# Gates of a graph network formed in pairs: the second 16 nodes added as differences on the first sums

## The chip, the cores and the metric

The kernel runs on one core of one Trainium2 chip. The core has a matmul engine (PE), a vector engine (DVE), an activation engine (ACT), a general engine (POOL), and a queue engine (SP) that issues most transfers. PE writes PSUM banks of 128 x 512 f32; DVE and ACT read and write PSUM and SBUF; POOL works on SBUF here. The metric is the device time of one execution in microseconds (us). Before the change it is 1396.1 us, the median of three runs (1394.9 to 1398.25).

## The reference, cut to what matters

The whole program is a stack of graph layers and feed-forward layers. Only the first part is touched, two graph layers, each followed by a gate between 256 nodes (8 graphs of 32) and 64 queries per graph, with 768 features:

```python
def _gate(h, q, Wg, bg, Wq, bq):
    B, L, F = q.shape                      # 8, 64, 768
    h3 = h.reshape(B, N, F)                # N = 32 nodes of a graph
    hg = einsum('bnf,gf->bng', h3, Wg[:, :F])
    qg = einsum('blf,gf->blg', q, Wg[:, F:]) + bg
    attn = sigmoid(hg[:, :, None, :] + qg[:, None, :, :])
    qi = einsum('bnlf,blf->bnf', attn, q)
    alpha = sigmoid(h3 @ Wq[:, :F].T + qi @ Wq[:, F:].T + bq)
    return alpha * tanh(qi) + (1 - alpha) * h3
```

For every graph, node, query and feature a sum of a node term and a query term goes through a sigmoid, is multiplied by the query and summed over the 64 queries.

## The kernel before, in words

**Units.** Features lie on the partitions. A unit is one graph `b` and one block `f` of 128 features; there are 48 in a layer. For a unit the gates are a tile of 128 x (32 nodes x 64 queries), f32, one of five buffers that `wtile` shares with a few other tiles. The first four graphs come graph by graph, the last four feature block by feature block.

**Forming a gate.** The sums are made by PE. `split3` cuts a projection into three bf16 parts that add up to the f32 value. `ga` holds two parts of a graph's 64 query terms in 128 rows; `gb` holds the third part in 64 rows and below it the three parts of 16 nodes in 48 rows, 112 rows in all, once for each half `u` of the nodes. Constant matrices of zeros and ones (`sela`, `selb`) pick a query and a node for each of 512 columns. `form` (L792) does two steps, one for each half: four matmuls (L798, L799) into a pair of PSUM banks `acc` (two such pairs rotate), then a sigmoid (L805) of 128 x 1024 into the gate tile.

**After it.** Units go by threes. For the first two of a triple POOL multiplies by the queries (L825); for the third ACT copies the 64 query columns into the PSUM bank `qy` ahead of its sigmoids (L822) and DVE multiplies (L832). `total` (L810) is DVE's sum over the queries. DVE's block for a triple is: the sum of the second unit of the triple before, the sum of the first unit of this one, the multiplication of the third unit, its sum.

**Work beside.** At each step of `form` the generator `beside` issues one more matmul over 384 columns in f32 on PE: in layer 0 the projections of later graphs (`q_terms` L582, `node_terms` L604), the alpha terms (`alpha_nodes` L632, `alpha_gates` L673), and products for the next layer (`z_beside` L644); in layer 1 less. From unit 22 of layer 0 on, the second step of a unit issues two. `alpha_gates` goes on only when the reductions that it needs were emitted five steps ago. What follows a projection (casts on ACT, L570 and L572, subtractions on DVE, L571 and L573, transfers by SP, L590 to L621) is emitted by `flush` a given number of steps later. `blend` puts three pieces for the first half of the nodes among the steps: transposes (L701), a tanh (L702), a subtraction (L705), sigmoids (L707), a multiplication and an addition (L711, L712). `z_beside` reads the blended nodes.

**Order.** `pin` keeps every instruction of this stage in program order on its engine, so a waiting instruction holds all behind it. Transfers on SP are placed by a planner. A node projection goes to `gb` over a DRAM tile (`rows`), apart from graph 0, which is copied from SBUF.

Of the kernel before, what the change touches and what calls it, by code (L numbers as in the profile page):

```python
# [18 lines left out]
P = 128  # L19
N = 256  # L20
NC = 2
D = 768
# [31 lines left out]
def graph_ffn_stack_kernel(ctx: ExitStack, tc: tile.TileContext, a: dict, out: bass.AP):  # L54
# [386 lines left out]
    with tc.tile_pool(name="g0", bufs=1) as g0, tc.tile_pool(name="g0t", bufs=2) as g0t, \  # L441
# [92 lines left out]


        gate_ctx = ExitStack()
        gt = gate_ctx.enter_context(tc.tile_pool(name="gate", bufs=1))
        ga = gt.tile([P, NB, D], BF16, name="ga")
        gb = gt.tile([P, 2, NB, D], BF16, name="gb")
        sela = gt.tile([P, 8, LQ], BF16, name="sela")  # L540
        selb = gt.tile([P, 2, 8, LQ], BF16, name="selb")
        nc.vector.tensor_copy(sela[0:64], ident[0:64, None, 0:64].to_broadcast([64, 8, LQ]))
        nc.vector.tensor_copy(sela[64:P], ident[64:P, None, 64:P].to_broadcast([64, 8, LQ]))
        id16 = ident[64:P, 64:P].rearrange("p (t n) -> p t n", t=4)
        nodes = gt.tile([P, 16], F32, name="nodes")
        nc.vector.tensor_tensor(nodes[64:P], id16[:, 0, :], id16[:, 1, :], OP.add)
        nc.vector.tensor_tensor(nodes[64:P], nodes[64:P], id16[:, 2, :], OP.add)
# [29 lines left out]
        def q_terms(w, c, i):  # L577

            fs = slice(i * 384, (i + 1) * 384)
            ps = side_bank("ps_qg")[:, :384]  # L580
            for k in range(KD):
                pin(nc.tensor.matmul(ps, qT[:, k, c * P:(c + 1) * P], w(k, i * 384, (i + 1) * 384),  # L582
                                     start=k == 0, stop=k == KD - 1))
# [12 lines left out]
            yield  # L596

        def node_terms(w, hT, c, i):

# [3 lines left out]
            for k in range(KD):  # L603
                pin(nc.tensor.matmul(ps, hT[:, k, c * P:(c + 1) * P], w(k, i * 384, (i + 1) * 384),  # L604
                                     start=k == 0, stop=k == KD - 1))
# [71 lines left out]
        def blend(hT, qiT, nT, qy, c):  # L677
# [67 lines left out]
        for layer in range(2):  # L745
# [3 lines left out]
            if layer == 0:  # L749
                run(q_terms(w_gb, 0, 0), q_terms(w_gb, 0, 1))  # L750
            gT = feature_tile("gT")
            for o in range(KD):
                ps = bank("ps_rgcn")[:, :N]
# [11 lines left out]
            nT = feature_tile("nT")  # L765
            qy = one_bank("qy", "ps_qy")
            if layer == 0:
# [3 lines left out]
                side[0] = 0  # L771
                beside = chained(lambda: q_terms(w_gb, 1, 1), lambda: node_terms(w_ga, gT, 1, 0),
                                 lambda: q_terms(w_gb, 2, 0), lambda: q_terms(w_gb, 3, 0),
                                 lambda: node_terms(w_ga, gT, 1, 1), lambda: q_terms(w_gb, 2, 1),
                                 lambda: q_terms(w_gb, 3, 1), lambda: pause(2), lambda: alpha_nodes(wa, gT, 0),
# [6 lines left out]
            else:  # L782
                run(node_terms(w_ga, gT, 1, 0))
                side[0] = 0
                beside = chained(lambda: node_terms(w_ga, gT, 1, 1), lambda: pause(10), lambda: alpha_nodes(wa, gT, 0),
                                 lambda: alpha_gates(wb, qiT, 0), lambda: blend(gT, qiT, nT, qy, 0),
# [4 lines left out]

            def form(b, f):  # L792
                fs = slice(f * P, (f + 1) * P)
                g = wtile("gate", (NPB, LQ))
                for u in range(2):
                    acc = acc2("gate_acc")
                    for i in range(2):
                        pin(nc.tensor.matmul(acc[:, i, :], ga[:, b, fs], sela, start=True, stop=False))  # L798
                        pin(nc.tensor.matmul(acc[:, i, :], gb[0:112, u, b, fs], selb[0:112, i], start=False, stop=True))  # L799
                    steps[0] += 1  # L800
                    next(beside, None)
                    if layer == 0 and u and n >= half * KD - 2:
                        next(beside, None)
                    flush()
                    pin(nc.scalar.activation(g[:, u * 16:(u + 1) * 16, :].rearrange("p n l -> p (n l)"),  # L805
                                             acc.rearrange("p a n -> p (a n)"), AF.Sigmoid, bias=bg[:, f:f + 1]))
                return g

# [8 lines left out]
            for n, (b, f) in enumerate(units):  # L817
                q = qT[:, f, b * LQ:(b + 1) * LQ]
                if n % 3 == 2:
                    at = (n // 3) % 4 * LQ  # L820
                    q_ps = qy[:, at:at + LQ]
                    pin(nc.scalar.copy(q_ps, q))  # L822
                g = form(b, f)
                if n % 3 != 2:
# [1175 lines left out]
```

## Time and profile before

| what | us |
|---|---|
| median of three runs (lowest to highest) | 1396.1 (1394.9 to 1398.25) |
| profiled execution, its own time | 1399.24 |
| its span, first to last instruction | 1397.2 |
| gate stage, layer 0: first POOL multiplication to last reduction | 140.13 to 310.48 |
| gate stage, layer 1: the same | 390.61 to 543.44 |
| busy over the span: PE, DVE, ACT, POOL | 1250.9, 672.2, 477.1, 360.5 |

In the rows of the page a group reads: line, engine, operation, output<-input with partitions x elements, count, then busy time and mean length in ns, then the idle time of the engine just before the group and what ended most of it. In a timeline a row starts with start and length in us, and the idle time before it stands in brackets with its releaser. In a row of busy time by stretch each engine has its busy us and its count; the clock of PE (1.00 is full), the share of the transfer engines and GB/s end the row.

### The profile page before, as it was taken

To read this page: it belongs to the slowest core of one execution; us is meant where nothing else is said; L and a number is where in the kernel's file an instruction comes from. 1 tells how busy PE (TensorE), PEld (TensorE's weight loads), DVE (VectorE), ACT (ScalarE), POOL (GpSimd) and SP (SyncE) were. 2 spreads that over 40 slices of the span, in tenths; PEclk is the share of its full clock that TensorE was granted. 3 is DMA by queue.
4 is the path that set the end of the run, shared out by engine and by line. 5 is a ranking of instruction groups with operands and counts; after the bars stand their busy time and mean duration, and the time that the engine had idled before them with its cause. 6 is when DMAs were issued, how large, how long until landed. Compare 5 with 4: busy or idle time off the path is not lost. (4 is left out here: it accounts for less than half of the span.)

```text
span 1397.2 us, 13979 instructions
## 1 busy us (share of the span) xinstructions
PE 1250.9 (90%) x5088; PEld 768.1 (55%) x5088; DVE 672.2 (48%) x1278; ACT 477.1 (34%) x826; POOL 360.5 (26%) x200
## 2 busy tenths in 40 slices
PE   7999999989998885799899978987879999878998
PEld 4567445446743432665545554545567545467854
DVE  4330899871079998315446271058262101365033
ACT  1012776551177763224114212215211111172122
POOL 1000998660089994000111201021011000100000
PEclk9999999999999996899999979998989999975989
DMA  9332160116240022150573139943019799801000
GB/s 345 115 120 95 43 183 19 68 57 237 79 125 0 0 102 77 52 198 7 192 282 128 53 110 371 364 183 102 23 63 348 291 395 401 338 1 36 32 0 23
DMA packets 78026, 197.70 MB, mean 142 GB/s; under 512 B 8828, under 2 KB 24288, under 8 KB 77824
## 3 DMA queue, kind: packets, MB, share of 16 engines
q1 hardware_dynamic: 69664, 163.06, 32.5%
q0 software_dynamic: 6576, 28.95, 5.9%
q10 hardware_dynamic: 1712, 4.72, 0.9%
q8 instruction: 44, 0.72, 0.2%
q14 instruction: 30, 0.25, 0.1%
HBM read 178.00 MB, written 15.27 MB: 138 GB/s over the span
## 5 line engine op out<-in xcount | busy, mean ns | idle before, releaser
L825 POOL TENSOR_TENSOR gate<-gate,qT 128x2048 f32<-128x2048 f32 x64 | 287.9, 4544 | 235.7 <-ACT gate L805 235.5
L805 ACT ACTIVATE gate<-gate_acc,bg 128x1024 f32<-128x1024 f32 x192 | 210.0, 1114 | 49.3 <-PE gate_acc L799 46.6
L810 DVE TENSOR_REDUCE qiT<-gate 128x32 f32<-128x2048 f32 x96 | 215.2, 2280 | 20.6 <-POOL gate L825 19.6
L798 PE MATMUL gate_acc<-sela,ga 128*128 128x512 bf16 x384 | 147.7, 385 | 24.2 <-ACT gate L805 23.8
L799 PE MATMUL gate_acc<-selb,gb 112*128 112x512 bf16 x384 | 148.0, 385 | 0.0
L1199 PE MATMUL up_acc<-w_e,xgT 128*64 128x384 f32 (+1 forms) x432 | 96.4, 489 | 0.0
L799 PEld LDWEIGHTS <-gb 112*128 112x128 bf16 x384 | 37.7, 98 | 94.6 <-issue 69.9
L832 DVE TENSOR_TENSOR gate<-gate,ps_qy 128x2048 f32<-128x2048 f32 x32 | 73.0, 2280 | 1.5 <-ACT gate L805 1.5
L1199 PEld LDWEIGHTS up_acc<-w_e,xgT 128*64 128x64 f32 (+1 forms) x432 | 46.9, 154 | 44.7 <-issue 27.3
L798 PEld LDWEIGHTS <-ga 128*128 128x128 bf16 x384 | 37.9, 99 | 48.1 <-issue 2.7
L673 PE MATMUL ps_alpha<-w_qb,qiT 128*128 128x384 f32 x96 | 42.0, 536 | 12.5 <-DVE qiT L810 12.5
L571 DVE TENSOR_TENSOR ps_hg<-ps_hg,hg 128x384 f32<-128x384 f32 x8 | 4.5, 562 | 96.7 <-ACT hg L570 96.7
L267 DVE CUSTOM_DVE_ANT_0 gat_dot<-xl,row 128x128 f32<-128x128 f32 (+2 forms) x56 | 23.8, 425 | 52.8 <-ACT xl L1577 18.9
L462 PE MATMUL ps_z<-w_rel,xT 128*128 128x384 f32 x144 | 47.9, 486 | 0.0
L1166 POOL DMA_INDIRECT yg<-ys,rows x8 | 7.6, 955 | 153.6 <-DMA w_qk<-in_L_ffn_W_qkvT 100.6
L1735 DVE TENSOR_TENSOR h<-up_acc,h 128x768 f32<-128x768 f32 x6 | 5.7, 958 | 80.1 <-PE up_acc L1199 80.1
L171 PE MATMUL ps_tr<-ident,xn 128*128 128x128 f32 x84 | 17.6, 377 | 29.0 <-DVE xn L160 14.1
L466 ACT COPY z<-ps_z 128x384 f32<-128x384 f32 x20 | 9.6, 479 | 90.2 <-PE ps_z L462 86.9
L102 PE MATMUL ps_e<-xT,w_s 128*128 128x256 f32 x144 | 36.4, 417 | 4.1 <-DVEq L1750 4.1
L632 PE MATMUL ps_alpha<-w_qa,gT 128*128 128x384 f32 x96 | 38.5, 496 | 0.7 <-ACT al L685 0.7
L1166 POOL DMA_INDIRECT xg<-table,slots x12 | 12.0, 1000 | 101.5 <-DVE gs L1640 37.7
L329 PE MATMUL ps_pt<-ident,gat_z 128*128 128x128 f32 x104 | 22.1, 344 | 16.6 <-DVE gat_s L321 16.6
(452 smaller groups left out, 2227.8 us busy)
## 6 DMA issues: line engine op xcount, KB each, us to landing
w_e<-in_L_ffn_W SPq DMA_DIRECT2D x32, 1152.0 KB, 12.4
w_rel<-in_L_gnn_W_rel SPq DMA_DIRECT2D x12, 1152.0 KB, 9.2
wi<-in_L_ffn_WiT SPq DMA_DIRECT2D x8, 1152.0 KB, 12.2
wo<-in_L_ffn_WoT SPq DMA_DIRECT2D x8, 1152.0 KB, 11.3
w_down<-in_L_ffn_W SPq DMA_DIRECT2D x8, 1152.0 KB, 11.0
w_s<-in_L_ffn_Ws SPq DMA_DIRECT2D x5, 1152.0 KB, 8.4
w_root<-in_L_gnn_W_root SPq DMA_DIRECT2D x4, 1152.0 KB, 11.3
w_ga<-in_L_gnn_WgAT SPq DMA_DIRECT2D x4, 1152.0 KB, 7.6
```

The source lines that it names most:

```text
L102: mm = nc.tensor.matmul(ps, w(k, lo, lo + P), xT[:, k, :], start=start and k == 0, stop=stop and k == kcs - 1)
L267: pin(nc.vector.tensor_tensor_reduce(t, xl[:, c, h * C:(h + 1) * C], r[:, h * C:(h + 1) * C], 1.0, 0.0, OP.mult, OP.add, accum_out=a2[:, w ...
L462: mm = nc.tensor.matmul(ps, hT[:, k, c * P:(c + 1) * P], w(k, i * 384, (i + 1) * 384), start=k == 0, stop=k == KD - 1)
L632: pin(nc.tensor.matmul(al_ps[c][i], hT[:, k, c * P:(c + 1) * P], w(k, i * 384, (i + 1) * 384), start=k == 0, stop=False))
L673: pin(nc.tensor.matmul(al_ps[c][i], qiT[:, f, c * P:(c + 1) * P], w(f, i * 384, (i + 1) * 384), start=False, stop=f == KD - 1))
L798: pin(nc.tensor.matmul(acc[:, i, :], ga[:, b, fs], sela, start=True, stop=False))
L799: pin(nc.tensor.matmul(acc[:, i, :], gb[0:112, u, b, fs], selb[0:112, i], start=False, stop=True))
L805: pin(nc.scalar.activation(g[:, u * 16:(u + 1) * 16, :].rearrange("p n l -> p (n l)"), acc.rearrange("p a n -> p (a n)"), AF.Sigmoid, bias ...
L810: pin(nc.vector.tensor_reduce(qiT[:, f, b * NPB:(b + 1) * NPB], g, AX.X, OP.add))
L825: pin(nc.gpsimd.tensor_tensor(g, g, q[:, None, :].to_broadcast([P, NPB, LQ]), OP.mult))
L832: pin(nc.vector.tensor_tensor(g, g, q_ps[:, None, :].to_broadcast([P, NPB, LQ]), OP.mult))
L1199: pin(nc.tensor.matmul(ps[at:at + n, :], xT[:, k, at:at + n], ws[r](k, lo, hi), start=start, stop=stop))
```

## The change

- A pair of units is formed together. The four steps of a pair are: first half of unit one, first half of unit two, second half of unit one, second half of unit two. Each unit keeps its own `acc` for both halves.
- The second half is no longer made from nothing. Its matmul adds, on top of the sums in PSUM, the difference between node 16 + n and node n: one matmul over 48 rows (`gd`, three bf16 parts of 16 differences) where there were two over 128 and 112 rows.
- `step_nodes` makes the node values for that on DVE before the projection (the first 16 nodes as they are, the second 16 minus the first), so `node_terms` projects these instead of `gT`. For the first half of the nodes they lie in a tile `d0`, for the second half in a part of `nT` that is not used yet.
- `gb` is kept once instead of twice; the differences go to `gd`, always by way of the DRAM tile, with rows 0 to 47 for even graphs and 64 to 111 for odd ones. A selector `seld` for rows 0 to 47 is added.
- ACT's copy of the queries stands behind the four sigmoids of a pair, not ahead of a unit's two.
- The tanh of the first blend goes to a tile of its own in SBUF (two buffers), no longer to the bank `qy`.

```diff
-        gb = gt.tile([P, 2, NB, D], BF16, name="gb")
+        gb = gt.tile([P, NB, D], BF16, name="gb")
+        gd = gt.tile([P, NB // 2, D], BF16, name="gd")
...
+        seld = gt.tile([64, 2, 8, LQ], BF16, name="seld")
...
+            nc.vector.tensor_copy(seld[:, i], nodes[0:64, i * 8:(i + 1) * 8, None].to_broadcast([64, 8, LQ]))
...
-                    for u in range(2):
-                        nc.sync.dma_start(gb[0:64, u, b, fs], parts[r, 2, :])
+                    nc.sync.dma_start(gb[0:64, b, fs], parts[r, 2, :])
...
+        def step_nodes(to, hT, c, o):
+            a, b = (t.rearrange("p (b u n) -> p b u n", b=4, u=2) for t in (hT[:, o, c * P:(c + 1) * P], to[:, o, :]))
+            nc.vector.tensor_copy(b[:, :, 0, :], a[:, :, 0, :])
+            nc.vector.tensor_tensor(b[:, :, 1, :], a[:, :, 1, :], a[:, :, 0, :], OP.subtract)
...
-                    for u in range(2):
-                        for s in range(3):
-                            nc.sync.dma_start(gb[64 + s * 16:80 + s * 16, u, 0, fs], parts[u * 16:(u + 1) * 16, s, :])
+                    for s in range(3):
+                        nc.sync.dma_start(gb[64 + s * 16:80 + s * 16, 0, fs], parts[0:16, s, :])
                 v = rows.rearrange("(j u n) s d -> u s n j d", j=4, u=2)
-                for u in range(2):
+                for s in range(3):
+                    nc.sync.dma_start(gb[64 + s * 16:80 + s * 16, c * 4 + j0:(c + 1) * 4, fs], v[0, s][:, j0:, :])
+                for o in range(2):
                     for s in range(3):
-                        nc.sync.dma_start(gb[64 + s * 16:80 + s * 16, u, c * 4 + j0:(c + 1) * 4, fs], v[u, s][:, j0:, :])
+                        nc.sync.dma_start(gd[o * 64 + s * 16:o * 64 + 16 + s * 16, c * 2:(c + 1) * 2, fs], v[1, s][:, o::2, :])
...
-                th = qy[:, at:at + 256].rearrange("p (k n) -> p k n", k=2)
+                th = (qy[:, at:at + 256] if c else gt.tile([P, 256], F32, name="th", bufs=2)).rearrange(
+                    "p (k n) -> p k n", k=2)
...
                 nc.scalar.activation(gT[:, o, :], ps, AF.Relu, bias=col(bias, o))
-            run(node_terms(w_ga, gT, 0, 0), node_terms(w_ga, gT, 0, 1))
+                step_nodes(d0, gT, 0, o)
+            run(node_terms(w_ga, d0, 0, 0), node_terms(w_ga, d0, 0, 1))
...
+            def form(pair):
+                gs = [wtile("gate", (NPB, LQ)) for _ in pair]
+                accs = [acc2("gate_acc") for _ in pair]
                 for u in range(2):
+                    for (b, f), g, acc in zip(pair, gs, accs):
+                        fs = slice(f * P, (f + 1) * P)
+                        h = slice(b % 2 * 64, b % 2 * 64 + 48)
+                        for i in range(2):
+                            if u == 0:
+                                pin(nc.tensor.matmul(acc[:, i, :], ga[:, b, fs], sela, start=True, stop=False))
+                                pin(nc.tensor.matmul(acc[:, i, :], gb[0:112, b, fs], selb[0:112, i],
+                                                     start=False, stop=True))
+                            else:
+                                pin(nc.tensor.matmul(acc[:, i, :], gd[h, b // 2, fs],
+                                                     seld[0:48, i] if b % 2 == 0 else selb[64:112, i],
+                                                     start=False, stop=True, skip_group_check=True))
+                        steps[0] += 1
                         next(beside, None)
+                        if layer == 0 and u and n >= half * KD - 2:
+                            next(beside, None)
+                        flush()
+                        pin(nc.scalar.activation(g[:, u * 16:(u + 1) * 16, :].rearrange("p n l -> p (n l)"),
+                                                 acc.rearrange("p a n -> p (a n)"), AF.Sigmoid, bias=bg[:, f:f + 1]))
+                return gs
...
+                if n % 2 == 0:
+                    pair = form(units[n:n + 2])
+                g = pair[n % 2]
                 if n % 3 == 2:
                     at = (n // 3) % 4 * LQ
                     q_ps = qy[:, at:at + LQ]
                     pin(nc.scalar.copy(q_ps, q))
-                g = form(b, f)
```

More of the change, by code (lines that the diff above doesn't have):

```diff
@@ L538, in graph_ffn_stack_kernel @@
         ga = gt.tile([P, NB, D], BF16, name="ga")
-        gb = gt.tile([P, 2, NB, D], BF16, name="gb")
+        gb = gt.tile([P, NB, D], BF16, name="gb")
+        gd = gt.tile([P, NB // 2, D], BF16, name="gd")
         sela = gt.tile([P, 8, LQ], BF16, name="sela")
         selb = gt.tile([P, 2, 8, LQ], BF16, name="selb")
+        seld = gt.tile([64, 2, 8, LQ], BF16, name="seld")
         nc.vector.tensor_copy(sela[0:64], ident[0:64, None, 0:64].to_broadcast([64, 8, LQ]))
         nc.vector.tensor_copy(sela[64:P], ident[64:P, None, 64:P].to_broadcast([64, 8, LQ]))
-        id16 = ident[64:P, 64:P].rearrange("p (t n) -> p t n", t=4)
         nodes = gt.tile([P, 16], F32, name="nodes")
-        nc.vector.tensor_tensor(nodes[64:P], id16[:, 0, :], id16[:, 1, :], OP.add)
-        nc.vector.tensor_tensor(nodes[64:P], nodes[64:P], id16[:, 2, :], OP.add)
+        for h in (slice(0, 64), slice(64, P)):
+            id16 = ident[h, h].rearrange("p (t n) -> p t n", t=4)
+            nc.vector.tensor_tensor(nodes[h], id16[:, 0, :], id16[:, 1, :], OP.add)
+            nc.vector.tensor_tensor(nodes[h], nodes[h], id16[:, 2, :], OP.add)
         for i in range(2):
@@ L591, in place, with node_terms @@
                     nc.sync.dma_start(ga[64:P, b, fs], parts[r, 1, :])
-                    for u in range(2):
-                        nc.sync.dma_start(gb[0:64, u, b, fs], parts[r, 2, :])
+                    nc.sync.dma_start(gb[0:64, b, fs], parts[r, 2, :])
             split3(ps, "qg", place)
             yield
-        def node_terms(w, hT, c, i):
+        def step_nodes(to, hT, c, o):
+            a, b = (t.rearrange("p (b u n) -> p b u n", b=4, u=2) for t in (hT[:, o, c * P:(c + 1) * P], to[:, o, :]))
+            nc.vector.tensor_copy(b[:, :, 0, :], a[:, :, 0, :])
+            nc.vector.tensor_tensor(b[:, :, 1, :], a[:, :, 1, :], a[:, :, 0, :], OP.subtract)
+        def node_terms(w, dT, c, i):
             fs = slice(i * 384, (i + 1) * 384)
@@ L603, in node_terms @@
             for k in range(KD):
-                pin(nc.tensor.matmul(ps, hT[:, k, c * P:(c + 1) * P], w(k, i * 384, (i + 1) * 384),
+                pin(nc.tensor.matmul(ps, dT[:, k, :], w(k, i * 384, (i + 1) * 384),
                                      start=k == 0, stop=k == KD - 1))
@@ L751, in graph_ffn_stack_kernel @@
             gT = feature_tile("gT")
+            d0 = wtile("d0", (KD, P))
             for o in range(KD):
@@ L765, in graph_ffn_stack_kernel @@
             nT = feature_tile("nT")
+            d1 = nT[:, :, P:]
+            for o in range(KD):
+                step_nodes(d1, gT, 1, o)
             qy = one_bank("qy", "ps_qy")
@@ L771, in graph_ffn_stack_kernel @@
                 side[0] = 0
-                beside = chained(lambda: q_terms(w_gb, 1, 1), lambda: node_terms(w_ga, gT, 1, 0),
+                beside = chained(lambda: q_terms(w_gb, 1, 1), lambda: node_terms(w_ga, d1, 1, 0),
                                  lambda: q_terms(w_gb, 2, 0), lambda: q_terms(w_gb, 3, 0),
-                                 lambda: node_terms(w_ga, gT, 1, 1), lambda: q_terms(w_gb, 2, 1),
+                                 lambda: node_terms(w_ga, d1, 1, 1), lambda: q_terms(w_gb, 2, 1),
                                  lambda: q_terms(w_gb, 3, 1), lambda: pause(2), lambda: alpha_nodes(wa, gT, 0),
@@ L782, in graph_ffn_stack_kernel @@
             else:
-                run(node_terms(w_ga, gT, 1, 0))
+                run(node_terms(w_ga, d1, 1, 0))
                 side[0] = 0
-                beside = chained(lambda: node_terms(w_ga, gT, 1, 1), lambda: pause(10), lambda: alpha_nodes(wa, gT, 0),
+                beside = chained(lambda: node_terms(w_ga, d1, 1, 1), lambda: pause(10), lambda: alpha_nodes(wa, gT, 0),
                                  lambda: alpha_gates(wb, qiT, 0), lambda: blend(gT, qiT, nT, qy, 0),
                                  lambda: pause(3), lambda: alpha_nodes(wa, gT, 1), lambda: alpha_gates(wb, qiT, 1))
-            def form(b, f):
-                fs = slice(f * P, (f + 1) * P)
-                g = wtile("gate", (NPB, LQ))
+            def form(pair):
+                gs = [wtile("gate", (NPB, LQ)) for _ in pair]
+                accs = [acc2("gate_acc") for _ in pair]
@@ L795, in form @@
                 for u in range(2):
[L796 to L802, printed above, removed]
-                        next(beside, None)
@@ L804, in form @@
[L804 to L807, printed above, removed]
+                    for (b, f), g, acc in zip(pair, gs, accs):
[11 more added lines that the diff above has]
+                        steps[0] += 1
+                        next(beside, None)
+                        if layer == 0 and u and n >= half * KD - 2:
[3 more added lines that the diff above has]
+                                                 acc.rearrange("p a n -> p (a n)"), AF.Sigmoid, bias=bg[:, f:f + 1]))
```

## The prediction, made before the changed kernel was run

> **What bounds the kernel now.** I read the groups of the page first, then busy time by stretch of the gate stage, then single engines around the stalls, last the matmul engine's raw order. The change touches the gate stage alone; it runs twice (layer 0 and layer 1).
>
> ```profile
> L825 POOL TENSOR_TENSOR gate<-gate,qT 128x2048 f32<-128x2048 f32 x64 | 287.9, 4544 | 235.7 <-ACT gate L805 235.5
> L805 ACT ACTIVATE gate<-gate_acc,bg 128x1024 f32<-128x1024 f32 x192 | 210.0, 1114 | 49.3 <-PE gate_acc L799 46.6
> L810 DVE TENSOR_REDUCE qiT<-gate 128x32 f32<-128x2048 f32 x96 | 215.2, 2280 | 20.6 <-POOL gate L825 19.6
> L798 PE MATMUL gate_acc<-sela,ga 128*128 128x512 bf16 x384 | 147.7, 385 | 24.2 <-ACT gate L805 23.8
> L799 PE MATMUL gate_acc<-selb,gb 112*128 112x512 bf16 x384 | 148.0, 385 | 0.0
> ```
>
> Three units (a triple) cost POOL two multiplications, 2 x 4.51 = 9.0 us; DVE three reductions and one multiplication, about 4 x 2.24 = 8.95 us; ACT six sigmoids, 6.7 us. POOL and DVE are nearly equal, so saving PE time counts only where PE is slower than 9 us a triple. Busy time by stretch (columns: PE, weight loads, DVE, ACT, POOL, clock, DMA):
>
> ```profile
> 140.00:205.00 65.00, 63.67 (x249) 31.46 (x248) 60.11 (x36) 51.59 (x63) 63.12 (x14) 1.00 0.36 110
> 205.00:238.00 33.00, 32.30 (x124) 16.41 (x123) 32.86 (x18) 22.39 (x26) 28.36 (x7) 1.00 0.18 43
> 238.00:262.00 24.00, 21.41 (x79) 10.93 (x78) 17.24 (x17) 14.16 (x22) 16.72 (x4) 0.93 0.28 99
> 262.00:310.00 48.00, 43.57 (x163) 22.23 (x161) 42.14 (x19) 28.26 (x33) 36.02 (x8) 0.99 0.12 41
> 391.00:544.00 153.00, 125.60 (x479) 57.09 (x478) 146.86 (x77) 107.45 (x123) 143.94 (x34) 0.96 0.15 48
> ```
>
> Layer 1 (last row) has POOL and DVE busy 94% and 96%: almost nothing to win. Layer 0 begins the same way (POOL 63.1 of 65), and only after 238 does POOL idle. The rest of layer 0 is where the change can pay. There, in the timeline, multiplications of a triple (L832) start 11.04 us apart (271.14, 282.18, 293.22), 2 us over POOL's pace; and around 238 to 262 the blend of the first half stalls everyone:
>
> ```profile
> 248.64 0.39 ACT L702 ACTIVATE ps_qy<-qiT 128x256 f32<-128x256 f32 x1 [4.75 <-DVE gate L832]
> ...
> 251.77 8.99 POOL L825 TENSOR_TENSOR gate<-gate,qT 128x2048 f32<-128x2048 f32 x2 [6.05 <-ACT gate L805]
> ...
> 255.38 0.42 DVE L705 TENSOR_TENSOR nT<-ps_qy,gT 128x256 f32<-128x256 f32 x1 [3.12 <-ACT ps_qy L822]
> ```
>
> The tanh writes the PSUM bank that the queries live in, so it waits for a DVE multiplication that only reads queries. DVE's idle gaps from 238 to 310 add up to 12.2 us: no more than that can be won in layer 0.
>
> **Removed: two of eight matmuls a unit.** Durations of 379 ns overlap; starts give the price:
>
> ```profile
> 160.84 0.38 PE L798 MATMUL gate_acc<-sela,ga 128*128 128x512 bf16 x1
> ...
> 161.71 0.81 PE L582 MATMUL ps_qg<-w_gb,qT 128*128 128x384 f32 x2
> ...
> 162.36 0.38 PE L798 MATMUL gate_acc<-sela,ga 128*128 128x512 bf16 x1
> ```
>
> Four gate matmuls take 161.71 - 160.84 = 0.87 us, 0.217 each; one f32 matmul of the work beside takes 0.65. A step after unit 22 averages 0.87 + 1.5 x 0.65 = 1.84, so a triple 11.04, as seen. Two matmuls less save 0.433 a unit.
>
> **Added: matmuls over 48 rows.** [...]
>
> ```profile
> 1195.87 1.45 PE L1160 MATMUL moe_acc<-w_s,gs 128*128 128x384 f32 x4
> 1197.26 0.91 PE L1162 MATMUL moe_acc<-b,cwT 9*128 9x384 f32 x2
> 1198.09 0.91 PE L1160 MATMUL moe_acc<-w_s,gs 128*128 128x384 f32 x2
> ...
> 1161.61 0.49 PE L1725 MATMUL up_acc<-b_rows,own 72*128 72x384 bf16 x2
> 1161.94 3.39 PE L1199 MATMUL up_acc<-w_e,xgT 128*128 128x384 f32 x10
> ```
>
> A record of 384 f32 columns normally takes 0.323 (2 x 0.323 = 0.65). Four before L1162 should end at 1197.16; it starts 0.10 late. Its two take 0.83 where 0.65 was due: 0.18. The pair after it reads 0.91 where the plain pair above reads 0.81: another 0.10. So a visit to a nine-row matmul costs 0.38; 72 rows (L1725, 0.33 for two of 0.16) cost nothing, and 48 lies on the nine-row side. With bf16 weights (98 ns to load against some 187 in f32) I take 0.32; bounds 0.18 (the two gaps alone) and 0.39. Every second-half step makes one visit, since work beside follows. Without the price of the rule, 24 units from 22 on would save 24 x 0.433 = 10.4 us; with it 24 x 0.113 = **-2.7 us** (bounds -6.1 and -1.0). In units 0 to 21 and in layer 1 POOL and DVE hide it: 0.
>
> **Pairs, start.** Three sigmoids run back to back from 137.93 and POOL starts at 140.13, after the second. In pairs the second sigmoid is unit 1's, so unit 0 is complete one sigmoid later: +1.1. In layer 1 likewise (390.61 now). With a small wait of the first DVE multiplication for the copy behind four sigmoids: **+2.4 us** for both; no cover, POOL and DVE being full from there on.
>
> **Pairs, first 22 units.** Splits of the projections flush every six steps: second cast (ACT), subtraction (DVE). Now four steps are emitted before DVE's block of a unit n=2 (mod 6). So at steps 18, 30, 42 two rounds of subtractions stand side by side, and the second waits for a cast that waits for the first: a cast of 0.48 plus two hops, 0.6 us of idle DVE where DVE is the bound, three times: **+1.8** (0 to 2.5). The cast stands ahead of two sigmoids on ACT, which have over 2 us of slack.
>
> **Tanh to SBUF.** Freed of the bank. It ends the 4.75 us wait above; the DVE gaps it can close are 1.98 + 3.12 in layer 0 and an ACT wait of 1.6 in layer 1. But the next item makes DVE late there anyway, so I take **-1.0 and -1.0** (bounds 0 and -6.7).
>
> **The third piece of the blend.** Counting steps: before, the last reductions of unit 22 are emitted at step 54, now with pair 26/27 at step 56, so the work beside reaches the blend two steps later. The blend's third piece (subtract, multiply, add, 1.25 us) stood at steps 71 and 72, just ahead of DVE's block for unit 35; now it is at 73 and 74, behind it. Two matmuls (L644, k = 4, 5) need it and stand in PE's order ahead of unit 38's gates. DVE: block of unit 32 from 241.95 + 3.7 (lost so far), 8.95, second piece 1.25, block of 35 8.95, third piece 1.25: done at 266.1. PE comes to k = 4 at about 262.4 now (k = 3 at 260.91, then a gate step); two steps later, less the freed tanh, the same. Stall **3.7**. Behind it wait unit 38's gates, so POOL and DVE.
>
> Then the clock:
>
> ```profile
> 247.80:251.10 3.30, 1.12 (x6) 0.60 (x5) 3.27 (x3) 2.43 (x5) 0.00 (x0) 1.00 0.59 182
> 251.20:254.60 3.40, 3.40 (x8) 1.40 (x8) 0.92 (x3) 2.27 (x4) 2.83 (x1) 0.52 0.39 157
> ```
>
> A stretch in which PE worked 1.12 of 3.30 us was followed by 3.4 us at half clock. [...] I follow the row: 4.2 us of work at half clock, **+2.1**. The piece in all +5.8 (0 to 7.5).
>
> **Nothing on the path.** Differences (24 small DVE instructions a layer, 0.15 to 0.28 each by L158 and L908, at most 6.7 us) fall in DVE's idle stretch of 33 us before 127.75, 57 before 378.08; the last needed is ready 0.6 after its relu (123.84), needed at 126.4. Uncovered: 0.6 a layer. The selector copies sit there too. SP: two issues fewer for each of eight query pieces, three more for each of four c=1 node pieces: -4 of about 0.5. Unit 0's differences now come by way of DRAM: rows issued 129.5, landed 131.9, six issues of 0.5, landing 1.9: 136.8, needed at 139.1; late, it would cost the excess once.
>
> **Sum:** 2.4 + 1.8 - 2.7 - 2.0 + 5.8 = +5.3. The profiled execution took 1399.24 (span 1397.2, 2.0 outside), 3.1 above the median 1396.1; the sum on it is 1404.5, on the median **1401.4 us**.
>
> **Rivals.** (A) As forecast, 57%: 1401.4, own range 1399 to 1405. (B) It is faster: a visit costs only 0.18 and PE gets to k = 4 after the third piece. Decisive is DVE's lag at unit 35: below 1.7 us of it there is no stall. Then 4.2 - 6.1 - 3.9 (tanh released in full) = -5.8, 1390.3. For it: POOL's 2 us idle a triple; against it: DVE has no idle gap before 238, so it comes late. 16%. (C) No stall, visits at 0.32: 4.2 - 2.7 - 2.0 = -0.5, 1395.6; 16%. (D) The clock falls widely: in layer 1 three matmul slots in four remain (1.7 of 3.4 us busy against 2.29 in 445 to 448.4, which kept full clock), and each half-clock stretch that meets work beside costs up to 1.7; four of them, +6: 1407.4; 11%. Against it: PE has slack in layer 1. That five buffers starve the pairs is in A's range: between a freed buffer and DVE's multiplication lie two reductions, 4.4 us, and three sigmoids, a copy and hops need 3.6.
>
> **Numbers.** Within 0.2% (2.8 us) this kernel's times can't be told from no change. Faster is B and an edge of C, 0.17; same is most of C and an edge of A, 0.18; slower is A and D, 0.65. B and D reach past both ends; 1391.5 to 1406.5 leaves one in ten on each side.
>
> **What would show it.** L798 192, L799 192 and the new line 192 records; after the new line a matmul starting some 0.2 late; POOL's first start 1.1 later; L644 waiting some 4 us for DVE near 262, and half clock after it. Wrong if triples from unit 38 on come under 9.8 us apart without such a wait, or if the new matmuls start at 0.217 with no gaps.

## The result, and where the time went

The changed kernel takes 1439.88 us (median of 4 runs, 1437.94 to 1440.21) where the kernel before, run beside it, took 1395.5 (1393.62 to 1398.25): a ratio of 1.0327, 95% interval 1.0286 to 1.0367. Slower was forecast, but by 5 us; it is 44. (Ratios and intervals here are formed from fast runs and are not the quotient of the two medians, so the two can differ a little.)

The profiled execution has a span of 1436.0 us against 1397.2. I divide it in four at GpSimd's first gate multiplication and the end of the last gate reduction of each layer, both read from the timelines: layer 0's gates 170.4 before, 181.2 after; between the layers 80.1 and 81.6; layer 1's gates **152.8 and 172.2**; and all that follows **853.7 and 861.0**. So 10.8 + 1.5 + 19.4 + 7.3 = 39.0 us are to be explained (the medians lie 44 apart: the profiled execution of before took 3.7 us more than its median, that of the change 1.9 less), half of them in layer 1, where the prediction saw "almost nothing to win" and nothing but the start to lose.

The groups of the changed kernel's page (columns: line, engine, operation, tiles and forms, count | busy us, mean ns | idle before it and what ended most of that):

```profile
L854 POOL TENSOR_TENSOR gate<-gate,qT 128x2048 f32<-128x2048 f32 x64 | 288.6, 4536 | 255.8 <-ACT gate L832 255.5
L832 ACT ACTIVATE gate<-gate_acc,bg 128x1024 f32<-128x1024 f32 x192 | 209.6, 1115 | 91.3 <-PE gate_acc L821 49.6
L837 DVE TENSOR_REDUCE qiT<-gate 128x32 f32<-128x2048 f32 x96 | 214.7, 2278 | 9.9 <-POOL gate L854 8.8
...
L821 PE MATMUL gate_acc<-selb,gb 112*128 112x512 bf16 x192 | 82.4, 429 | 1.5 <-issue 0.7
L820 PE MATMUL gate_acc<-sela,ga 128*128 128x512 bf16 x175 | 75.0, 429 | 6.5 <-ACT gate L832 6.3
...
L824 PE MATMUL gate_acc<-selb,gd 48*128 48x512 bf16 x96 | 31.9, 415 | 15.6 <-ACT gate L832 15.5
...
L824 PE MATMUL gate_acc<-seld,gd 48*128 48x512 bf16 x96 | 30.4, 399 | 12.7 <-ACT gate L832 12.6
```

Multiplications and reductions cost what they did before; GpSimd waits 20 us more (255.8, was 235.7), and the sigmoids' idle time went from 49.3 to 91.3. PE's saving is there: two lines of 192 full matmuls (17 records of L820 are missing) and 192 small ones, in place of two lines of 384. A mean of 429 ns against 385 says that more of them ran at half clock, where the record of one is 0.63 us and not 0.38 (those from 259.31 and from 135.13 on in this trace). Busy time by stretch (PE, weight loads, VectorE, ScalarE, GpSimd, clock, DMA), the last two rows longer since the stages are:

```profile
140.00:205.00 65.00, 60.20 (x193) 24.29 (x197) 57.84 (x37) 47.64 (x58) 59.23 (x14) 0.95 0.29 87
205.00:238.00 33.00, 31.59 (x108) 13.62 (x109) 32.85 (x16) 24.01 (x27) 31.27 (x8) 1.00 0.22 68
238.00:262.00 24.00, 17.50 (x58) 7.52 (x58) 22.12 (x14) 14.13 (x23) 17.75 (x4) 0.94 0.28 100
262.00:320.00 58.00, 46.02 (x146) 20.52 (x148) 44.20 (x23) 28.54 (x33) 36.12 (x8) 0.91 0.10 34
403.00:575.00 172.00, 127.65 (x373) 47.77 (x380) 163.96 (x77) 106.74 (x122) 144.62 (x34) 0.81 0.12 41
```

In layer 1 VectorE is busy 163.96 us, 17.1 more than before (146.86), though it has only as many gate instructions. VectorE's own timeline there shows what grew (start, duration, instruction, idle before):

```profile
505.54 1.88 DVE L718 TENSOR_TENSOR nT<-th,gT 128x256 f32<-128x256 f32 x1
507.52 0.42 DVE L724 TENSOR_TENSOR th<-ps_blend,nT 128x256 f32<-128x256 f32 x1
507.98 4.58 DVE L725 TENSOR_TENSOR nT<-th,gT 128x256 f32<-128x256 f32 x1
...
521.38 0.47 DVE L718 TENSOR_TENSOR nT<-th,gT 128x256 f32<-128x256 f32 x1
...
557.09 4.58 DVE L937 TENSOR_SCALAR before<-before_i 128x256 f32<-128x256 int32 x1 [0.53 <-POOL before_i L936]
```

and GpSimd's:

```profile
493.65 13.48 POOL L854 TENSOR_TENSOR gate<-gate,qT 128x2048 f32<-128x2048 f32 x3
507.76 4.52 POOL L854 TENSOR_TENSOR gate<-gate,qT 128x2048 f32<-128x2048 f32 x1 [0.63 <-ACT gate L832]
517.04 9.18 POOL L854 TENSOR_TENSOR gate<-gate,qT 128x2048 f32<-128x2048 f32 x2 [4.77 <-ACT gate L832]
...
557.03 4.50 POOL L854 TENSOR_TENSOR gate<-gate,qT 128x2048 f32<-128x2048 f32 x1
```

The blend's subtraction (L718) and addition (L725) took 0.42 us before, though GpSimd multiplied without a pause beside them:

```profile
399.94 107.87 POOL L825 TENSOR_TENSOR gate<-gate,qT 128x2048 f32<-128x2048 f32 x24 [0.32 <-ACT gate L805]
...
492.12 0.41 DVE L705 TENSOR_TENSOR nT<-ps_qy,gT 128x256 f32<-128x256 f32 x1
...
493.11 0.42 DVE L712 TENSOR_TENSOR nT<-ps_qy,gT 128x256 f32<-128x256 f32 x1
```

They differ from its product (L724, still 0.42) in one thing: since the tanh lies in SBUF, both their inputs do. Every one of them that starts while GpSimd multiplies (nine of twelve) ends 0.28 us after that multiplication: 507.14 and 507.42 for the first row shown, 512.28 and 512.56 for the third. The fourth, from 521.38 on, starts just before the end of one multiplication and is let in ahead of the next, which follows without a pause and takes 4.70 us for 4.52. In layer 1 the six sum to 15.3 us for 2.5; one `before` row (L937), which now falls beside a multiplication, takes 4.58 for 0.28. Together 17.1.

### The profile page after: what moved, and what is told of

It reads as the page before. It is cut to its first block, busy times and chain, and to the rows that moved or that the text cites. A ratio compares the mean times of both kernels' runs of the same rounds, so it can differ in the third digit from the quotient of the medians.

```text
span 1436.0 us, 13628 instructions
## 1 busy us (share of the span) xinstructions
PE 1250.9 (87%) x4879; PEld 745.5 (52%) x4896; DVE 702.7 (49%) x1330; ACT 476.4 (33%) x826; POOL 361.3 (25%) x200
## 5 line engine op out<-in xcount | busy, mean ns | idle before, releaser
L854 POOL TENSOR_TENSOR gate<-gate,qT 128x2048 f32<-128x2048 f32 x64 | 288.6, 4536 | 255.8 <-ACT gate L832 255.5
L832 ACT ACTIVATE gate<-gate_acc,bg 128x1024 f32<-128x1024 f32 x192 | 209.6, 1115 | 91.3 <-PE gate_acc L821 49.6
L821 PE MATMUL gate_acc<-selb,gb 112*128 112x512 bf16 x192 | 82.4, 429 | 1.5 <-issue 0.7
L820 PE MATMUL gate_acc<-sela,ga 128*128 128x512 bf16 x175 | 75.0, 429 | 6.5 <-ACT gate L832 6.3
L861 DVE TENSOR_TENSOR gate<-gate,ps_qy 128x2048 f32<-128x2048 f32 x32 | 72.9, 2278 | 6.4 <-ACT ps_qy L852 6.3
L824 PEld LDWEIGHTS <-gd 48*128 48x128 bf16 x192 | 12.5, 96 | 81.2 <-issue 79.9
L824 PE MATMUL gate_acc<-selb,gd 48*128 48x512 bf16 x96 | 31.9, 415 | 15.6 <-ACT gate L832 15.5
L1764 DVE TENSOR_TENSOR h<-up_acc,h 128x768 f32<-128x768 f32 x6 | 5.7, 958 | 80.1 <-PE up_acc L1228 80.1
L644 PE MATMUL ps_alpha<-w_qa,gT 128*128 128x384 f32 x96 | 43.7, 553 | 0.6 <-ACT al L697 0.6
L821 PEld LDWEIGHTS <-gb 112*128 112x128 bf16 x192 | 20.5, 107 | 40.7 <-issue 30.8
L824 PE MATMUL gate_acc<-seld,gd 48*128 48x512 bf16 x96 | 30.4, 399 | 12.7 <-ACT gate L832 12.6
L587 PE MATMUL ps_qg<-w_gb,qT 128*128 128x384 f32 x96 | 39.1, 516 | 1.0 <-DVE qg L578 1.0
```

The costliest lines, as they stand in the source:

```text
L644: pin(nc.tensor.matmul(al_ps[c][i], hT[:, k, c * P:(c + 1) * P], w(k, i * 384, (i + 1) * 384), start=k == 0, stop=False))
L821: pin(nc.tensor.matmul(acc[:, i, :], gb[0:112, b, fs], selb[0:112, i], start=False, stop=True))
L824: pin(nc.tensor.matmul(acc[:, i, :], gd[h, b // 2, fs], seld[0:48, i] if b % 2 == 0 else selb[64:112, i], start=False, stop=True, skip_gro ...
L854: pin(nc.gpsimd.tensor_tensor(g, g, q[:, None, :].to_broadcast([P, NPB, LQ]), OP.mult))
L861: pin(nc.vector.tensor_tensor(g, g, q_ps[:, None, :].to_broadcast([P, NPB, LQ]), OP.mult))
```

## The experiments

Fifteen kernels. Two theories to begin with: **P**, VectorE's two-input SBUF instructions are shut out while GpSimd works; **M**, the loss lies in the pairs, the 48-row matmuls and the clock.

**One part undone: the tanh back in the queries' bank.**

```diff
-                th = (qy[:, at:at + 256] if c else gt.tile([P, 256], F32, name="th", bufs=2)).rearrange(
-                    "p (k n) -> p k n", k=2)
+                th = qy[:, at:at + 256].rearrange("p (k n) -> p k n", k=2)
```

> The changed kernel with one part undone: the tanh of the first half's blend is written to the queries' PSUM bank again, not to SBUF. Theory P (a VectorE instruction whose two inputs both lie in SBUF has to wait while GpSimd multiplies; the subtraction and the addition of each piece became such instructions): each of the twelve takes 0.42 us again, layer 1's gate stage loses 12.8 us of its 172 and layer 0's some 5 of its 181, and the time is 1415 to 1424 us. Theory M (the pairs and the 48-row matmuls starve the sigmoids; the stretched blend only fills idle time): the blend's instructions may be short again, but the time stays within 4 us of 1440, or rises by about 2 because the bank's waits return.

Measured: 1418.26 us, 21.6 less. Layer 1's gates 156.1 (16.1 less), layer 0's 174.5 (6.7 less). VectorE's timeline, with GpSimd multiplying without a pause from 491.50 to 522.91:

```profile
498.31 0.41 DVE L717 TENSOR_TENSOR nT<-ps_qy,gT 128x256 f32<-128x256 f32 x1
498.82 0.43 DVE L723 TENSOR_TENSOR ps_qy<-ps_blend,nT 128x256 f32<-128x256 f32 x1
499.29 0.42 DVE L724 TENSOR_TENSOR nT<-ps_qy,gT 128x256 f32<-128x256 f32 x1
```

**That part alone, in the kernel before.** There is no room for another tile there, so the tanh goes to where the new features will be:

```diff
-                th = qy[:, at:at + 256].rearrange("p (k n) -> p k n", k=2)
                 old, new = hT[:, ks, cs], nT[:, ks, cs]
+                th = qy[:, at:at + 256].rearrange("p (k n) -> p k n", k=2) if c else new
```

> The kernel before with one thing of the change alone: the tanh of the first half's blend goes to SBUF (into the place of the new features, where the subtraction, the product and the sum then work). No pairs, no differences, no 48-row matmuls. Theory P: subtraction and addition of six pieces wait for what is left of a multiplication of 4.5 us, about 2 us each, twelve times, of which layer 0 hides some: 12 to 24 us slower than before, with single instructions of up to 4.6 us. Theory M: as the prediction's step had it, 0 to 2 us faster than before.

Measured: 1420.95 against 1396.8, ratio 1.018 (1.0147 to 1.0214); layer 1's gates 173.4 where 152.8 were, layer 0's 173.4 for 170.4. No pair, no 48-row matmul is in it. P holds from both sides. Its worst line of VectorE:

```profile
494.41 11.20 DVE L705 TENSOR_TENSOR nT<-nT,gT 128x256 f32<-128x256 f32 x1
```

and what GpSimd did meanwhile:

```profile
482.87 22.46 POOL L825 TENSOR_TENSOR gate<-gate,qT 128x2048 f32<-128x2048 f32 x5
```

Five multiplications without a gap end at 505.33, the subtraction at 505.61: it started in the third of them and was not let in after it or after the fourth. This is the exception. Of the changed kernel's nine held instructions five got in between two multiplications that follow each other without a pause; only here and once in the run with 112 rows (6.55 us) did one wait through a further multiplication, until GpSimd paused. So the wait is mostly the rest of one multiplication, but not bounded by it; what decides it, no run here shows.

**The 48 rows made 112.**

```diff
...
-                                pin(nc.tensor.matmul(acc[:, i, :], gd[h, b // 2, fs],
-                                                     seld[0:48, i] if b % 2 == 0 else selb[64:112, i],
+                                pin(nc.tensor.matmul(acc[:, i, :], gd[0:112, b // 2, fs], seld[0:112, b % 2, i],
...
```

(`seld` has two forms, zero where the other graph's rows stand.)

> The changed kernel with the second halves' matmuls over 112 rows in place of 48: both graphs of a pair of graphs stand in the weights, and zeros in the selector take the other one out. [...] Theory P: the PE time of 0.32 us a step counts only after unit 22 of layer 0, and there part of it goes into the wait for the third piece: 2 to 6 us faster than the changed kernel. Theory M: the visits are the main loss: more than 10 us faster, and layer 1 shorter too.

Measured: 1431.93, 7.9 less, layer 0 3.8 of it, layer 1 0.6; between the two expectations. The two stages explain 4.4 of it; the profiled execution, of 1437.43, took 5.3 us more behind the gates than that of the changed kernel. Other waits are left in it: VectorE idles 8.6 us in one piece before 278.5.

**The third piece of layer 0's blend ahead of the block of unit 35.**

```diff
-            first, gap = ((2, 3) if layer == 0 else (3, 9)) if c == 0 else (2, 0)
+            first, gap = ((2, 2) if layer == 0 else (3, 9)) if c == 0 else (2, 0)
```

> The changed kernel with the pieces of layer 0's first blend two steps apart in place of three, so that the third piece stands in VectorE's order ahead of the block of unit 35, as before the change. The prediction's step of the third piece (stall 3.7 and half clock 2.1, seen in the changed kernel as a wait of 7.9 us of a z matmul for the piece's product): 4 to 8 us faster than the changed kernel, all of it in layer 0. If the stall only takes the place of other waits there (rival): within 2 us of the changed kernel.

Measured: 1433.25, 6.6 less; layer 0's gates 174.4, 6.8 less, layer 1's the same. What it removed, in the waits of the changed kernel from 238 to 285 (total us, times, longest):

```profile
POOL gate L854 <- ACT gate L832: 19.8, 3, 17.0
ACT gate L832 <- PE gate_acc L821: 12.2, 5, 10.2
...
PE ps_z L656 <- DVE th L724: 7.9, 1, 7.9
```

A z matmul waits 7.9 us for the piece, the next gates stand behind it, and GpSimd is idle for 17.0 at a stretch. In this run that wait is gone and GpSimd's longest pause there is 8.3; part of it moved to a transposition that waits for the piece before (7.0 us, was 4.3).

**The query copies ahead of a pair's sigmoids again.** The two lines of the copy stand before `form(units[n:n + 2])`, for whichever of the two units is a triple's third.

> The changed kernel with the other part of the change undone alone: the query of a triple's third unit is copied to PSUM ahead of its pair's four sigmoids, not behind them. Theory Q (VectorE's multiplication waits for that copy at the late triples of layer 0, 2.3 us at two of them, and once at each layer's start): 3 to 7 us faster than the changed kernel's 1440. Rival: the multiplication waits for the sigmoid of its own second half anyway, which stands just ahead of the copy: within 2 us of 1440.

Measured: 1435.99, 3.9 less, which with runs of 1434.11 to 1442.63 is not clear of the noise; and theory Q's reason is not in it: layer 0's gates got **longer**, 185.1. ScalarE's timeline:

```profile
170.13 0.22 ACT L851 COPY ps_qy<-qT 128x64 f32<-128x64 f32 x1 [4.18 <-DVE gate L863]
170.28 3.12 ACT L832 ACTIVATE gate<-gate_acc,bg 128x1024 f32<-128x1024 f32 x3
```

The copy waits for the multiplication of the triple before, which reads the same tile (five such waits, 14.9 us, up to 240), and now four sigmoids stand behind it. So the pairs need the copies where the change put them. Layer 1 was 5.1 us shorter; where GpSimd pauses more, the blend's instructions can meet fewer multiplications, but I did not take that apart.

**The last 7 us: PE's instruction stream.** All that follows the gates is the same code, yet it takes 7.3 us more. The expert stage has one place that alone costs 5.8 more: PE comes to a conditional block that is jumped over. The line of the branch in the kernel before (x2: min/median/max ns, first and last start; the last is the jump):

```profile
L1493 PEldq COMPARE_BRANCH  x2: 98/255/412, 841.7 to 842.0; - x2
```

and in the changed kernel:

```profile
L1522 PEldq COMPARE_BRANCH  x2: 98/3139/6180, 870.2 to 870.5; - x2
```

The change took 192 matmuls and their weight loads, 384 instructions, out of PE's stream ahead of it. If the jump's time hangs on how many PE instructions stand ahead of it, 126 more may bring it back to about 0.4 us, and the time down by 4 to 6; that 126 is the number was the author's estimate. So I put 63 small matmuls in, where PE waits for VectorE anyway:

```diff
+                for _ in range(63 if k + j == 0 else 0):
+                    pin(nc.tensor.matmul(ps[:2, 0, 0:1], token, token[:, 0:1], start=True, stop=True))
                 for c in range(NC):
                     pin(nc.tensor.matmul(ps[:, j, :], xn[:, c, (k + j) * P:(k + j + 1) * P], at[:, c, :],
...
```

> The changed kernel with 63 matmuls of one column (126 PE instructions, about 2 us) put in front of the first-rows matmuls of the expert stage, where PE waits over 5 us for VectorE; nothing uses what they write. In the changed kernel PE's compare-and-branch behind that stage takes 6.2 us where it took 0.4 before, although it is the same instruction. [...] Rival (the branch waits for data or for another engine): it stays at 6 us, and the time is the same or up to 2 us longer.

Measured: the jump takes 304 ns again, and what follows the gates 854.2 us, 6.8 less (the median, 1429.31, is 10.6 lower). And the opposite, 65 such matmuls (130 instructions, again an estimate) in the kernel before, which should bring the jump to about 6 us and the time up by 4 to 6:

> The kernel before with 65 such matmuls (130 PE instructions) in the same place. [...] Rival: the branch stays at 0.4 us and the time within 2 us.

Measured: 1404.86 against 1397.45, ratio 1.0063 (1.0046 to 1.008); after the gates 859.9, 6.2 more, and

```profile
L1495 PEldq COMPARE_BRANCH  x2: 98/3119/6140, 837.0 to 837.3; - x2
```

The same code, moved by 130 instructions, jumps in 6.1 us in place of 0.4, and the changed kernel's, moved by 126, in 0.3 in place of 6.2: 5.7 and 5.9 us between the long and the short jump. So the number of instructions ahead of it moves it both ways; what makes a jump long, no trace here shows. The other kernels agree too: the jump takes 6.04 to 6.22 us in the six that have the 384 instructions less and no small matmuls, and in the kernel before with 65 of them; in the other ten it takes 0.30 to 0.41. For the rest of this stage one execution is a rough measure: with the jump short it took 850.3 us in one of the kernels below, where the granted clock was 0.91, and 862.5 in another, where it was 0.89.

**Everything mended at once.** First attempt: the tanh in the free half of the blend's own PSUM bank (a PSUM input, and free of the queries), pieces two steps apart, copies early.

```diff
...
-                    sg.append(one_bank(tag, "ps_blend")[:, :256].rearrange("p (k n) -> p k n", k=2))
+                    both = one_bank(tag, "ps_blend").rearrange("p (h k n) -> p h k n", h=2, k=2)
+                    sg.append(both[:, 0])
+                    if c == 0:
+                        th[0] = both[:, 1]
...
```

> The changed kernel with three mends at once: the tanh goes to the free half of the blend's own PSUM bank (so the blend has a PSUM input again, and doesn't wait for the queries' bank), layer 0's pieces stand two steps apart, the queries are copied ahead of a pair's sigmoids. Theory P with the third piece: 18 to 25 for the first, 4 to 7 for the second, 0 to 5 for the third: 1405 to 1417. What is left over the 1396 of before would be the branch's 5.8 and the pairs themselves. If the gains hide one another: 1415 to 1422, no better than the first mend alone.

Measured: 1440.2. None of it came (layer 0's gates 187.9). With the copies left behind the sigmoids and the branch mended:

> The changed kernel with everything mended that the runs so far name: the tanh in the free half of the blend's PSUM bank, layer 0's pieces two steps apart, the 63 small matmuls that put the branch back. The query copies stay behind the sigmoids. If the three causes are separate, their gains add: 21.6 + 6.7 + 7.2 from 1440, that is 1403 to 1408; what then remains over 1396 is the price of the pairs and differences themselves (about +10). If they overlap: 1410 to 1416.

Measured: 1422.65, not 1403 to 1408. It is 17.6 less than the first attempt, more than the branch gives, so the early copies were a loss there. And with 112 rows:

> The same with the second halves' matmuls over 112 rows, so that the visits to the 48-row mode go too. By the visit price of 0.32 a step, 24 steps after unit 22 and no cover: 4 to 8 us faster than the same kernel with 48 rows, 1396 to 1403. Rival: VectorE and GpSimd hide PE there: within 2 us of it.

Measured: 1404.52. The step from 48 to 112 rows is 18.1, but the version with 48 rows lies 15 to 20 us above what was expected of it, so something else costs time. Two kernels on the base of before tell what. The pairs alone (full second halves from `ga` and `gb`, nothing else of the change):

> The kernel before with the pairs alone: the second halves are made in full again (four matmuls, no differences), the tanh stays in the queries' bank, the copies stand behind a pair's sigmoids. The prediction's terms for the pairs: start 2.4, splits side by side 1.8, third piece with its half clock 5.8: 1400 to 1407. Rival: the pairs cost next to nothing and the loss lies in the 48-row matmuls and the clock: 1396 to 1398.

Measured: 1416.72, with a wide spread (1406.19 to 1424.63), ratio 1.0114 (1.0063 to 1.0165): by the ratio 9 to 23 us, where 4 to 11 were expected. The profiled execution, of 1424.63, has layer 0's gates at 181.7 (11.3 more than before) and layer 1's at 156.1 (3.3 more), but also 8.8 more behind the gates. A z matmul waits 4.7 us for the third piece, and GpSimd is idle for 12.2 us in one piece before 275.0. What else the pairs cost this run does not separate. And the tanh in the blend's bank alone:

> The kernel before with the tanh in the free half of the blend's own PSUM bank, and nothing else: freed of the queries' bank as by the change, without a second SBUF input for VectorE. The prediction's step for a freed tanh, -1 a layer, without the wait for GpSimd: 1392 to 1396. Rival: what the tanh gains is taken by the next wait, within 1 us of 1396.

Measured: 1414.2, ratio 1.0108 (1.0061 to 1.0154). So that mend was itself the loss. Its waits from 392 to 560:

```profile
ACT ps_blend L710 <- DVE nT L708: 14.7, 2, 8.5
```

The kernel before has no such wait in this stretch. The blend's sigmoids, in the bank that the subtraction reads, now wait for VectorE, and the gates' sigmoids wait behind them on ScalarE. With the tanh in the queries' bank, pieces two steps apart, the branch mended and 112 rows:

> As the mended kernel with 112 rows, but the tanh stays in the queries' PSUM bank and not in the blend's own (the run of the kernel before with the tanh in the blend's bank alone was 16.4 us slower than before, so that mend was itself a loss). If the terms add, some 10 to 16 us faster than the 1404.5 of the version with the blend's bank: 1388 to 1395, and so no slower than before. Rival (the blend's bank costs less beside the pairs, the pairs themselves cost the rest): 1398 to 1404.

Measured: 1397.3 against 1397.18, ratio 0.9982 (0.9961 to 1.0003); 7.2 less than with the blend's bank, where 10 to 16 were expected. The same with 48 rows:

> The same with the second halves over 48 rows as in the change. The tanh undone (21.6), the third piece (6.7) and the branch (7.2) from 1440, if they add: 1402 to 1407; against the version with 112 rows it shows what the mode visits cost with nothing else in the way: 0.32 times 24 steps, 7.7 us, by the prediction; 14 to 18 if layer 1 pays as well, as the pair of runs with the tanh in the blend's bank had it.

Measured: 1406.36, ratio 1.0076 (1.0053 to 1.0098); here the blend's bank had cost 16.3. 1439.88 - 21.6 - 6.6 - 6.8 = 1404.9: with this mend the three add (with the 10.6 that the branch gave by medians the sum is 1401.1, so this holds to some 5 us). The visits to 48 rows make 9.1, most of it in layer 0 (176.9 against 166.1; layer 1 157.5 against 155.1, the 48-row trace being of an execution of 1411.42). PE's timeline of the 48-row version, one pair from its first gate matmul to the next pair's:

```profile
280.28 0.38 PE L819 MATMUL gate_acc<-sela,ga 128*128 128x512 bf16 x1
...
283.41 0.60 PE L823 MATMUL gate_acc<-seld,gd 48*128 48x512 bf16 x2
283.94 1.56 PE L685 MATMUL ps_alpha<-w_qb,qiT 128*128 128x384 f32 x4
285.43 0.60 PE L823 MATMUL gate_acc<-selb,gd 48*128 48x512 bf16 x2
285.96 1.56 PE L656 MATMUL ps_z<-w_rel,nT 128*128 128x384 f32 x4
287.36 0.38 PE L819 MATMUL gate_acc<-sela,ga 128*128 128x512 bf16 x1
```

and with 112 rows:

```profile
271.29 0.38 PE L822 MATMUL gate_acc<-sela,ga 128*128 128x512 bf16 x1
...
277.78 0.38 PE L822 MATMUL gate_acc<-sela,ga 128*128 128x512 bf16 x1
```

7.08 us a pair against 6.49: two visits, 0.295 each. Last, the two small waits of the pairs:

```diff
...
-            later(6, lambda: pin(nc.scalar.copy(parts[:, 1, :], ps)))
-            later(7, lambda: pin(nc.vector.tensor_tensor(parts[:, 2, :], ps, parts[:, 1, :], OP.subtract)))
+            later(8, lambda: pin(nc.scalar.copy(parts[:, 1, :], ps)))
+            later(9, lambda: pin(nc.vector.tensor_tensor(parts[:, 2, :], ps, parts[:, 1, :], OP.subtract)))
...
```

(and, within a pair, the first unit's query copied right behind its second sigmoid)

> The version with 112 rows and the tanh in the queries' bank, and two small things more: the second rounding of a split comes eight steps behind the first in place of six, so that no two subtractions stand side by side in VectorE's order (the prediction's term of 1.8 us), and the query's copy for a pair's first unit stands behind that unit's second sigmoid, not behind the other unit's (its wait of 1.4 us at two late triples). 2 to 5 us faster than without them. Rival: the waits move on to GpSimd, within 1 us.

Measured: 1395.39, ratio 0.9992 (0.9972 to 1.0011). In its trace the gate stages are 163.8 and 154.3, against 166.1 and 155.1 without the two edits, and 170.4 and 152.8 before. What follows the gates took 858.5 in that execution (853.3 without them), so the whole shows no gain. With the jump at 304 ns it is not the branch. The granted clock differs: of the 5.2 us, 3.6 are lost within 95 us of the last reduction, and there it fell lower (first row without the two edits, second with them; columns as above):

```profile
620.00:635.00 15.00, 12.39 (x73) 7.55 (x73) 11.58 (x24) 7.80 (x30) 0.54 (x1) 0.89 0.46 166
620.00:635.00 15.00, 12.83 (x58) 7.60 (x56) 9.90 (x20) 7.12 (x27) 0.54 (x1) 0.66 0.34 133
```

Why it fell lower stays open. Mended, the idea is worth 6.6 us in layer 0 by one trace, against 1.5 in layer 1 and 1.4 between the layers, and as a whole it is not distinguishable from the kernel before.

The runs in one table (us; ratios to the kernel before run beside it, stages of the profiled execution divided as above; the two runs with the blend's bank beside the pairs and the first of all mends are left out):

| kernel | median | ratio | layer 0 | layer 1 | after |
|---|---|---|---|---|---|
| before | 1395.5 | | 170.4 | 152.8 | 853.7 |
| changed | 1439.88 | 1.0327 | 181.2 | 172.2 | 861.0 |
| tanh undone | 1418.26 | 1.015 | 174.5 | 156.1 | 859.8 |
| before, tanh in SBUF | 1420.95 | 1.018 | 173.4 | 173.4 | 850.0 |
| changed, 112 rows | 1431.93 | 1.024 | 177.4 | 171.6 | 866.3 |
| changed, third piece earlier | 1433.25 | 1.0255 | 174.4 | 171.9 | 864.4 |
| changed, copies early | 1435.99 | 1.0296 | 185.1 | 167.1 | 861.4 |
| changed, 63 small matmuls | 1429.31 | 1.0227 | 181.3 | 172.2 | 854.2 |
| before, 65 small matmuls | 1404.86 | 1.0063 | 170.3 | 152.9 | 859.9 |
| before, pairs alone | 1416.72 | 1.0114 | 181.7 | 156.1 | 862.5 |
| before, tanh in the blend's bank | 1414.2 | 1.0108 | 177.6 | 164.3 | 858.6 |
| mended, 48 rows | 1406.36 | 1.0076 | 176.9 | 157.5 | 854.2 |
| mended, 112 rows | 1397.3 | 0.9982 | 166.1 | 155.1 | 853.3 |
| the same, two small waits less | 1395.39 | 0.9992 | 163.8 | 154.3 | 858.5 |

## The prediction, step by step

- **Tanh to SBUF, "-1.0 and -1.0 (bounds 0 and -6.7)": the step that failed, in sign and by 24 us.** It asked only what the tanh would no longer wait for, and not what its readers would cost; the bounds excluded a loss without a reason. Undone it gives 21.6, alone it costs 24. With the wait that the runs then showed, for the rest of a GpSimd multiplication of 4.5 us, the estimate would have been twelve waits of half a multiplication, 2.2 us each, some 26 us in place of -2: the right size (though not every one of the twelve waited, and two waits, of 11.20 and 6.55 us, outlasted one GpSimd instruction). The kernel before gives a hint: VectorE's gate multiplications read their query from PSUM (L832, `ps_qy`) and GpSimd's do not (L825, `qT`). Beside that, rival B releases 3.9 "in full" where the bound has 6.7; nothing hangs on it.
- **Not in the sum: the branch, +5.8.** "Removed: two of eight matmuls" costed their time and not their place in the stream. The profile of before has two jumps of PE, of 0.41 and 3.79 us, but nothing that says what moves one; it belongs in the range of a change that adds or removes PE instructions ahead of a jump.
- **The third piece, +5.8: right in kind, near in size.** The wait for it was put at 3.7; with the tanh undone it is 3.1 (the weights of a z matmul waiting for the product), with the pairs alone 4.7, and 7.9 in the changed kernel, where the wait for GpSimd makes VectorE later still. Moved ahead, 6.6 come back, with that lateness in it. Half clock stood on both sides of it: the gate matmuls from 259.31 and from 270.59 on start 0.43 apart, where those from 135.13 on start 0.217 apart. Ahead of them PE was idle for 4.3 and 7.9 us. Whether a stall of 3.7, or a stretch in which PE is busy for a third, is enough for that, this run does not show; the +2.1 was the author's estimate from the one stretch of before.
- **48-row visits, 0.32 each: right.** That 48 rows would cost like nine and not like 72, on which the -2.7 rests, was the author's estimate, since the kernel before has no matmul over 48; the runs showed 0.295 by the pairs' period (7.08 with 48 rows, 6.49 with 112). From start to start, 0.42 for 0.32 on entering, 0.31 for 0.22 on leaving, 0.43 for 0.32 over the first f32 matmul after. Times 24 that is 7.1 for the 9.1 measured (from unit 22 on there are 26 units, not 24, which makes it 7.7; layer 1, put at 0, has a part too). The net of -2.7 is not measured by itself: the changed kernel without its tanh has layer 0's gates at 174.5, the pairs with full second halves at 181.7, but in an execution of 1424.63 where the median is 1416.72.
- **Pairs, first 22 units, +1.8: right.** Three VectorE gaps of 0.55 ahead of 162.49, 182.80 and 203.10 and one of 0.57 ahead of 204.23; eight steps in place of six removed them.
- **Start, +2.4: too much.** GpSimd starts at 139.97 (140.13 before): it does wait for one sigmoid more, but the gates' first matmul itself stands 1.2 us earlier. Between the layers 1.5 were lost.
- **Rival D, the clock.** From 403 to 575 it fell to 0.81, where 391 to 544 had 0.96. Its price is small: the mended kernel with 48 rows has 0.84 from 400 to 540 and layer 1 at 157.5, with 112 rows 0.88 and 155.1.
- **Late triples.** The multiplication waits 2.33 us for the copy at two of them, which the sum did not have; with 112 rows 1.44.

## What to carry to other kernels

Before a value is moved from PSUM to SBUF, look at who reads it: here a VectorE instruction whose inputs were then both in SBUF waited for the end of what GpSimd was doing (up to 4.58 us for 0.42, twice longer, 6.55 and 11.20), and a chain with twelve such steps, nine of them held, took 21.6 us more beside a busy GpSimd. A PSUM tile shared to get out of one wait brought the waits of its other user (14.7 us in layer 1 with the tanh in the blend's bank), so ask which engine's queue will stand behind the new wait. When time appears far from the edit, compare the branch instructions before looking for contention (here 5.8 us of 7.3).

## What the runs showed of the hardware

- A two-input SBUF instruction of VectorE that started beside a GpSimd multiplication of 4.5 us ended 0.28 us after one each time. In the changed kernel it got in ahead of a next multiplication that followed without a pause five times of nine, and that one then took 4.70; in other runs it twice waited through further ones (11.20 and 6.55 us for 0.42). A conversion with one SBUF input (L937, int32 to f32) was held too, once, 4.58 for 0.28; the reductions (96, of 2.27 to 2.29) and the instructions with a PSUM input (L861 2.27 to 2.29, L724 0.42 to 0.43) were not in that trace.
- A jump of PE over a block it does not execute took 0.30 to 0.41 us in ten kernels and 6.04 to 6.22 in seven, with 126 to 384 PE instructions more or less ahead of it; a second one later took 3.2 to 3.8 in every run (3.79 before, 3.63 in the changed kernel).
- One visit to 48 rows in the mended kernel took 0.10 us on the way in, 0.09 on the way out and 0.10 in the next f32 matmul; over 112 rows these were not there.
